# Layer 1's experts: the first matrix as the stationary operand, fetched for each block

## Chip, cores and metric

The kernel runs on one core of a Trainium2 chip. The metric is the device time of one execution in microseconds; the median of three runs is compared. One further execution was recorded by the hardware profiler, and all durations of single instructions come from it.

## What is computed

The reference is a decoder of two layers on 32 sequences of 100 tokens with 256 features, all in float32. Each layer has self-attention, cross-attention over a context of 361 rows, and a feed-forward part. The change concerns only the last part of all, the mixture of experts of layer 1, on 3200 tokens:

```python
def _L1_ffn_ref(x, shared_w1, shared_w2, experts_w1, experts_w2, gate_w):
    ...
    shared = jnp.einsum('td,dh->th', x_flat, shared_w1.T)
    shared = jnp.einsum('th,hd->td', jax.nn.silu(shared), shared_w2.T)
    gate_logits = x_flat @ gate_w.T
    top_k_gates, top_k_idx = jax.lax.top_k(gate_logits, TOP_K)
    top_k_gates = jax.nn.softmax(top_k_gates, axis=1)
    ...
    h = jnp.einsum('td,ehd->teh', x_flat, experts_w1)
    expert_out = jnp.einsum('teh,edh->ted', jax.nn.silu(h), experts_w2)
    selected = jnp.einsum('ted,te->td', expert_out, gates)
    return (shared + selected).reshape(B, S, D)
```

There are 8 experts with a hidden width of 1024. Each token uses two of them, with gates from a softmax over its two largest logits, and a shared expert works on every token.

## The kernel before

Everything ahead of layer 1's feed-forward part is left as it is. The tokens are normalized and gated while layer 1's cross-attention runs; an indirect DMA (`send`) puts each token's row, with its gates and its number, twice into `sorted_dram`, once for each of its experts, so that the rows of one expert lie together. What follows has two stages, each with its order of instructions written out by hand for PE, DVE, ACT and SP (`in_order(SP)`).

**The stage of the shared expert** (the pool `f1s`) walks over 13 chunk pairs h of 256 tokens (the last has 128) times 8 slices m of the hidden width. `hidden` (its matmuls are booked on L208, inside `project`) multiplies a slice of the first matrix, as the stationary operand, by the turned tokens; ACT applies the silu (L1839); `added` multiplies by the second matrix (L1847). The stage begins with `rows_of`, which loads normalized rows (`xn`, L1799), and `rows_turned`, which turns them on PE (L1812). Along the way SP loads the experts' matrices: all eight first matrices into `wx1` (64 KB in each partition, L1928) and all eight second matrices into `wx2` (L1969). `blocks_of` works out which expert each block belongs to (`number`) and where its rows start (`rows_at`), and `get` fetches the first blocks' rows (`xg`, L1778). Some constants (L1748 to L1761: `ti`, `ones8`, `pi`, `empty` and others) are made by POOL in the pool `f1r`, which is opened after `wx1`. `empty` is written to the spare rows of `acc_dram` (L1914) and `sorted_dram` (L1915).

**The stage of the experts** (the pool `f1u`) walks over TILES = 57 blocks of 128 rows, each of one expert; which one is only known from a register. For each block:

- `get` (SP) fetches the rows, four blocks ahead, into one of six buffers `xg`;
- `turned` (PE L1982, DVE L1986) turns the rows into `xgT`, two blocks ahead;
- `first` (PE L208, `sc<-wx,xgT`) has the turned rows as the stationary operand and 512 columns of the first matrix as the moving one, at an address in `wx1` that a register gives; ACT's silu (L2000) writes `h`, with tokens in the partitions;
- `hidden_turned` turns `h` with eight transposes on PE (L2009) into `hgT`; ACT (L2015) and DVE (L2017) copy one half each out of PSUM;
- `second` (PE L208, `po<-wx,hgT`) multiplies by the second matrix of the expert; DVE scales by the gate into `y` (L2032, three buffers); POOL's indirect DMA (L2033) adds the rows to `acc_dram`. Each such scatter waits for the one before it, and a buffer `xg` is free only when its scatter has ended, since the scatter reads the row numbers in it.

The loop sets the order on every engine:

```python
for t in range(-2, TILES):
    if 0 <= t + 4 < TILES and t >= 0:
        get(t + 4)
    if t + 2 < TILES:
        turned(t + 2)
    if t >= 0:
        hidden_turned(t)
    if 0 <= t + 1 < TILES:
        first(t + 1)
    if t >= 0:
        second(t)
```

At the end `acc_dram` is copied to the output.

Of the kernel before, what the change touches and what calls it, by code (L numbers as in the profile page):

```python
# [10 lines left out]
F32 = mybir.dt.float32  # L11
# [3 lines left out]
AF = mybir.ActivationFunctionType  # L15
# [3 lines left out]
P = 128  # L19
# [7 lines left out]
E = 8  # L27
HID = 1024
NTOK = B * T
NCH = NTOK // 128  # L30
TILES = (2 * NTOK + E * 127) // 128
# [35 lines left out]
def kernel(ctx: ExitStack, tc: tile.TileContext, io: dict, out: bass.AP):  # L67
    nc = tc.nc
# [22 lines left out]
    def mm_tile():  # L91
        return psum["mm"][1].tile([P, 512], F32, tag="mm", name="mm")
# [5 lines left out]
    ident = const.tile([P, P], F32, name="ident")  # L98
# [395 lines left out]
    w1 = open_weights(1)  # L494
# [584 lines left out]
    with tc.tile_pool(name="a1", bufs=2) as pool, tc.tile_pool(name="a1p", bufs=1) as fixed:  # L1079
# [4 lines left out]
        for k, shift in enumerate((np.pi / 2, 0.0)):  # L1084
            a = fixed.tile([P, 16], F32, tag=f"ang{k}", name=f"ang{k}")
            t = fixed.tile([P, 16], F32, tag=f"turns{k}", name=f"turns{k}")
# [14 lines left out]
        for c in range(2):  # L1101
            ps = mm_tile()
# [5 lines left out]
        ps = mm_tile()  # L1108
# [629 lines left out]

    wx1_cm = tc.tile_pool(name="wx1", bufs=1, side="right")
    wx1_pool = wx1_cm.__enter__()
    wx1 = wx1_pool.tile([P, E, 2, HID], F32, name="wx1")
    fixed_cm = tc.tile_pool(name="f1r", bufs=1, side="right")
    fixed = fixed_cm.__enter__()
    w1s, w2s = loaded
# [20 lines left out]
    number = fixed.tile([1, TILES], I32, name="number1")  # L1767
# [2 lines left out]
    blocks_cm = tc.tile_pool(name="f1t", bufs=2, side="right")  # L1770
    blocks = blocks_cm.__enter__()
    xgs = {}

    def get(t):

        xg = blocks.tile([P, ROW], F32, tag="xg", name="xg", bufs=6)
        at = nc.sync.value_load(rows_at[0:1, t : t + 1], min_val=0, max_val=E * RG)
        load = nc.sync.dma_start(xg, sorted_dram[bass.ds(at, P), :])  # L1778
        for put in sent:
            tc.add_manual_dep(  # L1780
                load.ins, put.name,
                mybir.DependencyInfo(
                    mybir.DependencyClass.Sync, mybir.DependencyReason.DATA
                ),
                reason="all rows are there",
            )
        xgs[t] = xg

    with tc.tile_pool(name="f1s", bufs=2, side="right") as pool, in_order(SP):
# [28 lines left out]
        def chunks(h):  # L1818
            return range(2 * h, min(2 * h + 2, NCH))
# [36 lines left out]
        def store(h):  # L1856
            n = len(chunks(h))
            nc.sync.dma_start(
                acc_dram[256 * h : 256 * h + n * P, :].rearrange("(c p) d -> p c d", p=P),
                accs.pop(h)[:, :n, :],  # L1860
            )
# [62 lines left out]
        for n in range(len(units) + 2):  # L1924
            if n < len(units):
                h, m = units[n]
                if m == 2 and 0 < h < E + 1:
                    nc.sync.dma_start(  # L1928
                        wx1[:, h - 1], io["f1_w1"][h].rearrange("(c p) n -> p c n", p=P)
                    )  # L1930
                if m == 4 and h % 2 == 1 and h // 2 + 1 < NB:
                    rows_turned(h // 2 + 1)
                    if h // 2 + 2 < NB:
                        rows_of(h // 2 + 2)
                hidden(h, m)
            if n >= 2:
                added(*units[n - 2])
            if n >= 8 and n % 8 == 4:
                store(n // 8 - 1)
                if n // 8 + 2 < NHB:  # L1940
                    sum_rows(n // 8 + 2)
            if n in (4, 8, 12, 14):
                gating(pool, NG - 1, {4: 2, 8: 3, 12: 4, 14: 5}[n])
            if n == 18:
                blocks_of()
            if n >= 16 and n % 2 == 0 and n < 32:

                nc.gpsimd.tensor_copy(pace, hTs[units[n]][0:1, 0:1])
                for k in range(2):
                    b = B - G + (n - 16) // 2  # L1950
                    if n < 24:
                        put(send(b, k))
                    else:
                        e = n - 24 + k
                        put(nc.gpsimd.indirect_dma_start(
                            sorted_dram[:, :],
                            bass.IndirectOffsetOnAxis(ap=rest[:, e : e + 1], axis=0), empty, None,
                        ))
            if n == 40:

                xpool_cm.__exit__(None, None, None)
                norms_cm.__exit__(None, None, None)
                early_cm.__exit__(None, None, None)
                wx2_cm = tc.tile_pool(name="wx2", bufs=1)
                wx2_pool = wx2_cm.__enter__()
                wx2 = wx2_pool.tile([P, E, 8, D], F32, name="wx2")
            if n >= 42 and n % 6 == 0 and n // 6 < 7 + E:
                e = n // 6 - 7
                nc.sync.dma_start(  # L1969
                    wx2[:, e], io["f1_w2"][e + 1].rearrange("(c p) n -> p c n", p=P)  # L1970
                )
            if n == 92:
                for t in range(4):
                    get(t)
        store(NHB - 1)
    with tc.tile_pool(name="f1u", bufs=2, side="right") as pool, in_order(SP):
        xgTs, hgTs, experts_ = {}, {}, {}

        def turned(t):
            pt = mm_tile()  # L1980
            for c in range(2):
                nc.tensor.transpose(  # L1982
                    pt[:, c * P : (c + 1) * P], xgs[t][:, c * P : (c + 1) * P], ident
                )
            xT = blocks.tile([P, 2, P], F32, tag="xgT", name="xgT")
            nc.vector.tensor_copy(xT.rearrange("p c t -> p (c t)"), pt[:, : 2 * P])  # L1986
            xgTs[t] = xT
            experts_[t] = nc.tensor.value_load(number[0:1, t : t + 1], min_val=0, max_val=E - 1)

        def first(t):  # L1990

            e, xT = experts_[t], xgTs.pop(t)
            ps = sc_tile()
            for n in range(2):
                project(
                    ps[:, n, :], [xT[:, c, :] for c in range(2)],
                    [wx1[:, bass.ds(e, 1), c, n * 512 : (n + 1) * 512] for c in range(2)],
                )
            h = pool.tile([P, HID], F32, tag="h", name="h")
            nc.scalar.activation(h, ps.rearrange("p a b -> p (a b)"), AF.Silu)  # L2000
            hgTs[t] = h

        def hidden_turned(t):
            h = hgTs[t]
            hT = pool.tile([P, 8, P], F32, tag="hgT", name="hgT")
            for n in range(2):
                pt = mm_tile()
                for m in range(4):
                    nc.tensor.transpose(  # L2009
                        pt[:, m * P : (m + 1) * P], h[:, (4 * n + m) * P : (4 * n + m + 1) * P],  # L2010
                        ident,
                    )
                dst = hT[:, 4 * n : 4 * n + 4, :].rearrange("p m t -> p (m t)")
                if n == 0:
                    nc.scalar.copy(dst, pt)  # L2015
                else:
                    nc.vector.tensor_copy(dst, pt)  # L2017
            hgTs[t] = hT

        def second(t):  # L2020
            e, hT, xg = experts_.pop(t), hgTs.pop(t), xgs.pop(t)
            po = po_tile()
            project(
                po[:, :D], [hT[:, m, :] for m in range(8)],
                [wx2[:, bass.ds(e, 1), m, :] for m in range(8)],
            )
            g = pool.tile([P, 1], F32, tag="gx", name="gx")
            ge = pool.tile([P, E], F32, tag="ge", name="ge")
            nc.vector.tensor_tensor(ge, xg[:, D : D + E], onehot[:, t, :], ALU.mult)
            nc.vector.tensor_reduce(g, ge, AX.X, ALU.add)  # L2030
            y = pool.tile([P, D], F32, tag="y", name="y", bufs=3)
            nc.vector.tensor_scalar(y, po[:, :D], g, None, ALU.mult)  # L2032
            nc.gpsimd.indirect_dma_start(  # L2033
                acc_dram[:, :],
                bass.IndirectOffsetOnAxis(
                    ap=xg[:, D + E : ROW].bitcast(U32), axis=0
                ),
                y, None, compute_op=ALU.add,
            )

        for t in range(-2, TILES):
            if 0 <= t + 4 < TILES and t >= 0:
                get(t + 4)
            if t + 2 < TILES:
                turned(t + 2)
            if t >= 0:
                hidden_turned(t)
            if 0 <= t + 1 < TILES:
                first(t + 1)
            if t >= 0:  # L2050
                second(t)
# [2 lines left out]
    wx2_cm.__exit__(None, None, None)  # L2054
    blocks_cm.__exit__(None, None, None)
    fixed_cm.__exit__(None, None, None)
    wx1_cm.__exit__(None, None, None)
    close_weights(5)
    share_psum()

# [119 lines left out]
```

## Time and profile before

| | |
|---|---|
| median of 3 runs | 3895.03 us (3892.2 to 3896.37) |
| the profiled execution | 3894.81 us, of which its span is 3893.1 |
| busy in the span | PE 3583.1, PEld 2250.5, DVE 2034.2, ACT 1523.8, POOL 1338.3 us |
| stage of the shared expert | from about 3225 to 3417 us of the span |
| loop over the blocks | from 3419.2 to 3875.6 us |
| output copied | from 3880 us to the end |

PE is TensorE's matmuls, PEld its weight loads, which overlap the matmuls; DVE, ACT, POOL and SP are VectorE, ScalarE, GpSimd and SyncE. A line of a timeline gives the start and the duration in microseconds, then engine, line of the kernel, operation and the tiles as output<-inputs, with the number of instructions merged; what stands in square brackets is the idle time ahead of it and what ended it. The end of a matmul is modelled by the profiler, so that the recorded durations of neighbours overlap; the distance from one start to the next is the time that a matmul takes in a row. A tile's buffer number is left out, so `wx` stands for both `wx1` and `wx2`. "q" behind an engine marks its queue issuing a DMA.

### The profile page before, as it was taken

What the parts mean: (1) busy time and instruction counts of PE and PEld (TensorE: products, weight loads), DVE (VectorE), ACT (ScalarE), POOL (GpSimd) and SP (SyncE); (2) the same over time, 40 slices, a digit from 0 to 9 for tenths busy, and PEclk for the clock granted to TensorE, in tenths of its full rate; (3) what the DMA queues carried; (4) which work ended last, traced back from release to release, by engine and by line L of the source; (5) the groups of instructions that cost most, each with busy time, mean ns of one, the idle gap of its engine ahead of it and who ended that gap; (6) DMA issues with size and microseconds to landing.
All of it is one profiled execution on the core that took longest, in us unless ns stands there. A gap on an engine that the chain in (4) does not pass through costs nothing. (4 is left out here: it accounts for less than half of the span.)

```text
span 3893.1 us, 65394 instructions
## 1 busy us (share of the span) xinstructions
PE 3583.1 (92%) x25610; PEld 2250.5 (58%) x25610; DVE 2034.2 (52%) x5647; ACT 1523.8 (39%) x3254; POOL 1338.3 (34%) x941
## 2 busy tenths in 40 slices
PE   7888999996889899799999999999999998999998
PEld 5665565654545453333356666666666667867665
DVE  6776666654677766565544554645545552012221
ACT  4554555552322220456644444444444442222111
POOL 3334666664444532101122333332333332011211
PEclk9999999998899999899999999999999999999999
DMA  2001000000000000100100000000000004412222
GB/s 79 2 2 58 18 20 20 18 5 15 1 1 1 1 1 0 42 1 1 34 9 16 19 21 22 17 23 19 21 23 18 26 11 145 163 31 34 34 35 58
DMA packets 86508, 103.70 MB, mean 27 GB/s; under 512 B 13374, under 2 KB 79494, under 8 KB 85610
## 3 DMA queue, kind: packets, MB, share of 16 engines
q1 hardware_dynamic: 71532, 80.80, 7.1%
q0 software_dynamic: 12688, 15.36, 2.4%
q8 instruction: 205, 3.36, 0.4%
q10 hardware_dynamic: 1982, 3.35, 0.3%
q14 instruction: 101, 0.83, 0.1%
HBM read 74.02 MB, written 28.71 MB: 26 GB/s over the span
## 5 line engine op out<-in xcount | busy, mean ns | idle before, releaser
L1600 POOL TENSOR_TENSOR ex<-ex,rc 100x1444 f32<-100x1444 f32 x128 | 331.5, 2590 | 633.5 <-DVE rc L1599 631.0
L1591 ACT ACTIVATE ex<-s,nmx 100x361 f32<-100x361 f32 x512 | 303.1, 594 | 284.8 <-DVE nmx L1582 228.9
L364 POOL TENSOR_TENSOR s<-s,nmx 100x800 f32<-100x800 f32 x128 | 194.7, 1522 | 375.3 <-DVE nmx L363 372.0
L1199 ACT ACTIVATE h<-sc,cols 128x800 f32<-128x800 f32 x256 | 222.1, 923 | 135.1 <-PE sc L1193 134.8
L208 PE MATMUL mm<-f_we,x1T 128*100 128x512 f32 x512 | 265.5, 649 | 4.3 <-DVE x L1009 2.2
L2033 POOL DMA_INDIRECT acc_dram<-y,xg x57 | 88.8, 1557 | 494.3 <-DVE y L2032 342.8
L1582 DVE CUSTOM_DVE_ANT_0 s<-sc,mb 100x361 f32<-100x361 f32 x512 | 250.3, 526 | 0.7 <-PE sc L1575 0.6
L1575 PE MATMUL sc<-kT,qT 64*100 64x361 f32 x1024 | 206.3, 480 | 46.3 <-DVE vb L1563 30.7
L208 PE MATMUL po<-wx,hgT 128*128 x912 | 206.3, 379 | 0.3 <-ACT hgT L2015 0.3
L208 PE MATMUL sc<-wx,xgT 128*128 x456 | 205.2, 593 | 0.8 <-DVE xgT L1986 0.8
L208 PEld LDWEIGHTS po<-wx,hgT 128*128 128x128 f32 x912 | 173.3, 190 | 47.8 <-issue 26.8
L2032 DVE TENSOR_SCALAR y<-po,gx 128x256 f32<-128x256 f32 x57 | 27.6, 484 | 330.9 <-PE po L208 330.9
L1548 PE MATMUL sc<-x_wa,cT 128*128 128x512 f32 (+1 forms) x512 | 188.2, 490 | 0.0
L1022 DVE SCALAR_TENSOR_TENSOR x<-mm,wt,x 100x256 f32<-100x256 f32 x256 | 123.6, 483 | 114.2 <-PE mm L208 107.7
L376 PE MATMUL mm<-ident,ex 100*100 100x100 f32 x1024 | 126.5, 262 | 58.9 <-ACT eT L385 22.9
L1625 PEld LDWEIGHTS po<-eT,vb 128*64 128x64 f32 (+1 forms) x3072 | 140.2, 140 | 69.0 <-issue 68.6
L1518 PE MATMUL mm<-cT,x_wa 128*128 128x361 f32 x512 | 176.3, 467 | 0.0
L171 POOL TENSOR_TENSOR rs<-va,neghalf 100x4 f32<-100x4 f32 (+1 forms) x96 | 92.9, 970 | 220.1 <-DVE va L170 218.2
L385 ACT COPY eT<-mm 100x400 f32<-100x400 f32 x192 | 92.3, 492 | 193.9 <-PE mm L376 193.7
L1607 PE MATMUL mm<-ident,ex 100*128 100x100 f32 (+1 forms) x1536 | 164.3, 257 | 4.2 <-POOL ex L1600 4.1
L1614 ACT COPY eT<-mm 128x400 f32<-128x400 f32 (+1 forms) x256 | 125.9, 492 | 105.6 <-PE mm L1607 105.5
L1625 PE MATMUL po<-eT,vb 128*64 128x100 f32 (+1 forms) x3072 | 165.9, 258 | 0.0
(347 smaller groups left out, 7607.0 us busy)
## 6 DMA issues: line engine op xcount, KB each, us to landing
wx<-in_f_w SPq DMA_DIRECT2D x16, 1024.0 KB
xg<-sorted_dram SPq DMA_DIRECT2D x57, 132.5 KB
cb<-in_ctx SPq DMA_DIRECT2D x32, 192.0 KB
cT<-in_ctxT SPq DMA_DIRECT2D x32, 180.5 KB
cT<-in_ctxT SPq DMA_DIRECT2D x64, 90.2 KB
x<-in_x SPq DMA_DIRECT2D x8, 400.0 KB
x_dram<-x SPq DMA_DIRECT2D x32, 100.0 KB
xn_dram<-x SPq DMA_DIRECT2D x8, 400.0 KB
```

What stands on the lines that cost most here:

```text
L208: nc.tensor.matmul(ps, lhsT[k], rhs[k], start=(k == 0), stop=(k == n - 1))
L364: nc.gpsimd.tensor_tensor(sm, sm, bc(nmx, 2, T), ALU.add)
L376: nc.tensor.transpose(pt[:T, j * T : (j + 1) * T], exs[s, r // 2][:, 4 * (r % 2) + j, :], ident[:T, :T],)
L1199: nc.scalar.activation(h1, both[r2][:, :, :GT], AF.Tanh, bias=col("a1_b1", o))
L1518: nc.tensor.matmul(kTs[u][c][:, :S2], x1_wa[:, m * P : (m + 1) * P], cT[:, 0, :], start=True, stop=False,)
L1548: nc.tensor.matmul(ps[:kn, e, :n], cT[:, 0, at], x1_wa[:, 1024 + c0 : 1024 + c0 + n], start=True, stop=False,)
L1575: nc.tensor.matmul(ps[:T, e, :S2], qT[p0 : p0 + 64, m, tok], kT[p0 : p0 + 64, c, :], start=True, stop=True,)
L1582: nc.vector.tensor_tensor_reduce(s[:, e, :], ps[:T, e, :S2], mb, 1.0, 3.4e38, ALU.add, ALU.min, nmx[:, e : e + 1],)
L1591: nc.scalar.activation(ex[:, 2 * c + e, :], s[:, e, :], AF.Exp, bias=nmx[:, e : e + 1], scale=-1.0, accum_out=sm[:, 2 * c + e : 2 * c + e ...
L1600: nc.gpsimd.tensor_tensor(ex, ex, bc(rc, 2, S2), ALU.mult)
L1607: nc.tensor.transpose(pt[:kn, j * T : (j + 1) * T], ex[:, j, k0 : k0 + kn], ident[:T, :T])
L1625: nc.tensor.matmul(po[64 * e : 64 * e + 64, m * T : (m + 1) * T], vb[k][:kn, 256 * (u % 2) + 64 * h : 256 * (u % 2) + 64 * h + 64], eT[:kn ...
```

## The change

The first product of an expert's block is computed the other way round. Slices of 128 columns of the first matrix become the stationary operand and the turned rows the moving one, so that the product comes out with the hidden width in the partitions, as the second product needs it. The silu writes `hgT` directly, and `hidden_turned` with its transposes and two copies is gone. Each block's first matrix (1 MB) is fetched anew from memory by SP, at an address that a register gives (`first_matrix`), three blocks ahead into one of four buffers `w1b`; the tile `wx1` and its eight loads during the shared expert's stage are gone. With `wx1` gone, the pool `f1r` and what follows it lie at other addresses.

```diff
-    wx1_cm = tc.tile_pool(name="wx1", bufs=1, side="right")
-    wx1_pool = wx1_cm.__enter__()
-    wx1 = wx1_pool.tile([P, E, 2, HID], F32, name="wx1")
...
+    w1_of = {}
+
+    def first_matrix(t):
+
+        e = nc.sync.value_load(number[0:1, t : t + 1], min_val=0, max_val=E - 1)
+        w1 = blocks.tile([P, 2, HID], F32, tag="w1b", name="w1b", bufs=4)
+        nc.sync.dma_start(
+            w1, io["f1_w1"][1 : E + 1][bass.ds(e, 1)].rearrange("o (c p) n -> p (o c) n", p=P)
+        )
+        w1_of[t] = w1
...
-                if m == 2 and 0 < h < E + 1:
-                    nc.sync.dma_start(
-                        wx1[:, h - 1], io["f1_w1"][h].rearrange("(c p) n -> p c n", p=P)
-                    )
...
             if n == 92:
                 for t in range(4):
                     get(t)
+                    if t < 3:
+                        first_matrix(t)
...
         def first(t):
 
-            e, xT = experts_[t], xgTs.pop(t)
+            w1, xT = w1_of.pop(t), xgTs.pop(t)
             ps = sc_tile()
-            for n in range(2):
+            for m in range(8):
                 project(
-                    ps[:, n, :], [xT[:, c, :] for c in range(2)],
-                    [wx1[:, bass.ds(e, 1), c, n * 512 : (n + 1) * 512] for c in range(2)],
-                )
-            h = pool.tile([P, HID], F32, tag="h", name="h")
-            nc.scalar.activation(h, ps.rearrange("p a b -> p (a b)"), AF.Silu)
-            hgTs[t] = h
-
-        def hidden_turned(t):
-            h = hgTs[t]
+                    ps[:, m // 4, m % 4 * P : m % 4 * P + P],
+                    [w1[:, c, m * P : (m + 1) * P] for c in range(2)],
+                    [xT[:, c, :] for c in range(2)],
+                )
             hT = pool.tile([P, 8, P], F32, tag="hgT", name="hgT")
-            for n in range(2):
-                pt = mm_tile()
-                for m in range(4):
-                    nc.tensor.transpose(
-                        pt[:, m * P : (m + 1) * P], h[:, (4 * n + m) * P : (4 * n + m + 1) * P],
-                        ident,
-                    )
-                dst = hT[:, 4 * n : 4 * n + 4, :].rearrange("p m t -> p (m t)")
-                if n == 0:
-                    nc.scalar.copy(dst, pt)
-                else:
-                    nc.vector.tensor_copy(dst, pt)
+            nc.scalar.activation(
+                hT.rearrange("p m t -> p (m t)"), ps.rearrange("p a b -> p (a b)"), AF.Silu
+            )
             hgTs[t] = hT
...
         for t in range(-2, TILES):
             if 0 <= t + 4 < TILES and t >= 0:
                 get(t + 4)
+            if 3 <= t + 3 < TILES:
+                first_matrix(t + 3)
             if t + 2 < TILES:
                 turned(t + 2)
-            if t >= 0:
-                hidden_turned(t)
             if 0 <= t + 1 < TILES:
                 first(t + 1)
```

## The prediction

> **What bounds the kernel now.** I read the rows of busy tenths first, then the table of stages for the loop over expert blocks and for the stretch before it, then the groups by shape in that loop, then one block in order of time.
>
> ```profile
> PE   7888999996889899799999999999999998999998
> ...
> GB/s 79 2 2 58 18 20 20 18 5 15 1 1 1 1 1 0 42 1 1 34 9 16 19 21 22 17 23 19 21 23 18 26 11 145 163 31 34 34 35 58
> ```
> ```profile
> 3419.20:3875.60 456.40, 455.13 (x1934) 319.12 (x1934) 98.13 (x282) 91.68 (x114) 87.21 (x56) 1.00 0.21 32
> ```
> ```profile
> 3300.00:3400.00 100.00, 100.00 (x477) 88.25 (x476) 6.89 (x10) 23.21 (x59) 0.00 (x0) 1.00 0.52 175
> ```
> The columns of the last two lines are the stretch, its length, busy time of PE, PEld, DVE, ACT and POOL, granted clock, DMA share and GB/s. The block loop lasts 456.4 us and PE is busy 455.1 of them at full clock; DVE, ACT and POOL are each busy under a quarter, and the DMA engines 21%. PE bounds this loop. A busy PE could hide waits, so I check the spacing of one block:
>
> ```profile
> 3503.67 0.38 PE L1982 MATMUL mm<-ident,xg 128*128 128x128 f32 x2
> 3503.89 1.04 PE L2009 MATMUL mm<-ident,h 128*128 128x128 f32 x8
> 3504.63 1.55 POOL L2033 DMA_INDIRECT acc_dram<-y,xg  x1 [6.42 <-DVE y L2032]
> 3504.76 3.60 PE L208 MATMUL sc<-wx,xgT 128*128 x8
> 3508.19 3.62 PE L208 MATMUL po<-wx,hgT 128*128 x16
> 3508.56 0.33 SPq L1778 DMA_DIRECT2D xg<-sorted_dram  x1
> 3511.65 0.38 PE L1982 MATMUL mm<-ident,xg 128*128 128x128 f32 x2
> ```
> From start to start, two transposes of the rows take 0.22 us, eight transposes of the hidden values 0.87, the first product's eight passes 3.43 (0.429 each), the second product's sixteen 3.46 (0.216 each): 7.98 us, with no hole. One FP32 matmul stands in the trace as two passes. Whatever changes the block's time has to change PE's passes, or make PE wait.
>
> **What the Trainium skill says.** "TensorE: Matmul & The Clock Gate", section "LDWEIGHTS (loading the stationary operand)", prices a load by its columns: 128 columns at 1.2 per ns, an estimated 107 ns. The trace books 190 ns for one, but loads start closer than that. The same page, "Back-to-back issue gap", says that a stream of load and matmul pairs is paced by both, which is the question here. "DMA: Bandwidth & Descriptors", "Issuing engines are not separate DMA queues", says that all DMAs share the 16 engines, so the new fetches and the scatters meet there. Its "Queues, rings and completion order" has each engine change between queues only after a whole packet of descriptors. No view of before shows that sharing at the new load.
>
> **The change, part by part.**
>
> *First product.* Removed: 4 matmuls of 512 columns, 8 passes x 0.429 = 3.43 us a block. Added: 8 x 2 matmuls of 128 columns, 32 passes. The columns streamed are the same, 32 x 128 = 8 x 512, but there are 32 weight loads for 8, and a load may no longer hide under a pass. The nearest rows:
>
> ```profile
> 1581.36 0.97 PEld L208 LDWEIGHTS mm<-xm,a_w 128*128 128x128 f32 x8 [2.26 <-DVE xm L1151]
> ```
> ```profile
> 3411.88 0.61 PE L208 MATMUL mm<-xT,w 128*128 128x128 f32 x4
> ...
> 3412.33 0.60 PE L1847 MATMUL sc<-w,hT 128*128 128x256 f32 x2
> ...
> 3412.76 0.61 PE L208 MATMUL mm<-xT,w 128*128 128x128 f32 x4
> ```
> Eight full loads with 4-column matmuls, so with nothing to hide under, span 0.97 us: (0.97 - 0.19) / 7 = 0.111 us each. That is the pace of loads alone, near the page's 107 ns, and the booked 190 ns overlap. The second fence has the very shape of the new passes, in the shared expert's last half chunk: 4 of them take 3412.33 - 3411.88 = 0.45 us, 0.112 each. I take 0.111: 32 x 0.111 = 3.55 us, so **+0.12 a block**. Bounds: 0.107 (0.429 / 4, no cost of the extra loads) gives 0.00, and 0.1125 gives +0.17.
>
> *Transposes of the hidden values* (`hidden_turned`): 8 x 0.109 = **-0.87 us a block**, all on PE's path.
>
> *Evacuations.* ACT's copy (0.585) and DVE's copy (0.691) of each block go; the silu keeps its 1024 elements (1.02 us) and writes the turned form at once. ACT and DVE were never waited for in the steady block, so this is worth nothing there. Its cover is the second product of the block before (3.46 us) ahead of the silu's reader; were it gone, 1.0 us would show.
>
> *Fetching the matrix.* SP issues, per block, a register load, register arithmetic and a 1 MB transfer more. Six `get` in a row are issued within 5.79 us (from 3400.09 in SP's timeline), 1.1 us each; a fetch has one register sum more, so both make some 2.4 of a block's 7.2. Removed: eight 1 MB issues at 3231 to 3345, where PE did not wait for them. The loop before held 0.21 DMA share; 1.05 MB at 175 / 0.52 = 337 GB/s adds 3.1 us per block. Together (0.21 x 7.98 + 3.1) / 7.23 = 0.66 of the DMA engines. The order of instructions puts `first_matrix(t + 3)` on SP right behind `get(t + 4)`, which waits for the scatter of block t - 2; SP's gather at 3508.56 follows the y of 3504.35 by 4.2 us. Hence the fetch goes out about 5 us into block t - 1 and is needed at the start of `first(t + 3)`, three blocks on: 3 x 7.23 - 5 = 17 us for a transfer of about 3 to 6. **Cost 0**, by that cover. Queued behind SP's wait are only the next gather and fetch, with the same lead. The first three fetches go out from 3401, between the gathers, 15 us before the loop; also covered.
>
> *Scatter.* It must finish before the next one starts. POOL's issue at 3504.63 to SP's release by 3508.56 is 3.9 us, in a period of 8.0. If it stood behind a whole fetch it would take 3.9 + 3.1 = 7.0, still under 7.23, but barely.
>
> *Fill and drain.* The 57 blocks last 456.5 us, from the first pass at 3419.16 to the last y at 3875.64; 57 x 7.98 = 454.9, so 1.6 are edges, of which 0.99 is PE waiting for the first silu ahead of L2009 and goes. After: 57 x (0.22 + 3.55 + 3.46 = 7.23) = 412.1, with 0.5 of edges 412.6. **-43.9 us.**
>
> *The seam ahead of the shared expert.* Without the 64 KB `wx1`, the constants (L1748 to L1761) lie where memory is free early: the order shows POOL's seven instructions (1.3 us together) behind the memset of L1100, where POOL then idles 13.97 us, and `acc_dram<-empty` ahead of SP's first context loads (0.34 us there, used 18 us later). Both cost nothing. At the seam SP's first `xn` load no longer stands behind the last `x_dram` store:
>
> ```profile
> 3227.24 0.43 SPq L1799 DMA_DIRECT2D xn<-xn_dram  x1
> ...
> 3233.30 1.09 PE L1812 MATMUL mm<-ident,xn 128*128 128x128 f32 x4 [8.57 <-DMA xn<-xn_dram]
> ```
> PE waits 8.57 us for it. It can be issued near 3225.2, when the last tiles of the stage before come free: **-2 us** (0 to -2.5); next to be late is the rest of the same load.
>
> *Sum*: -43.9 - 2 = -45.9. The profiled execution took 3894.8 (span 3893.1 and 1.7 around it), 0.2 under the median of the runs, so 3895.0 - 45.9 = **3849**. With the bounds: pace 0.107 and the whole seam 3841, pace 0.1125 and no seam 3854.
>
> **Rivals.**
> *Slower, by the scatter.* It shares the DMA engines with a fetch that is new in every block, and the scatters are a serial chain. If one takes over 8.0 us instead of 3.9, POOL's chain sets the block and the kernel is slower; at 9.0 it is 57 x 1.0 = +57, 3952. For it: the chain lies on POOL and DMA, and a fetch ahead of it is new. Against: 3.9 + 3.1 = 7.0 needs the worst meeting each time. A chance of 4 in 100; a chain of 7.3 to 7.9 only eats part of the gain, 3855 to 3887, and with late fetches at the loop's start I give that 12 in 100.
> *Slower, by the weight loads.* If loads in a long row ran at the booked 0.190, the first product would take 6.08 and the block 9.76: +1.78 x 57 = +101, 3996. It decides from (8.01 - 3.46 - 0.22) / 32 = 0.135 a pass. The row of eight at 0.111 speaks against it; 32 in a row are not in the trace. 3 in 100.
> *No difference.* The gain of 0.76 a block is lost to waits by chance: 2 in 100.
> The likeliest case, PE bound at 7.2 to 7.3 a block, keeps 79 in 100.
>
> **How the numbers follow.** 3849 is the likeliest case. The range 3840 to 3864 holds it and the mildest of the partial losses, up to 0.25 us a block (57 x 0.25 = 14 above the sum). A measurement of this kernel tells about 0.2%, 8 us, from no change: faster 0.91, within 0.02, slower 0.07.
>
> **What would show it.** Right: blocks 7.2 to 7.3 apart, the new passes 0.111 apart, L2009 gone, PE with no wait for the fetched tile, PE's wait at the seam near 6.5. Wrong: passes over 0.13 apart; PE or PEld waiting for `w1b`; `acc_dram` scatters over 7 us apart from y to release, or y waiting for a scatter.

## The result, and the profile after

The changed kernel takes 3851.9 us (median of 5 runs, 3843.5 to 3857.1), the kernel before 3895.7 beside it (5 runs, 3892.2 to 3900.2). The ratio is 0.9885, with a 95% interval from 0.9869 to 0.9901: 43.8 us less, where the prediction had 45.9 less. The profiled execution of the changed kernel took 3857.05 (span 3855.3); it is the slowest of the five, so its span is not read as the kernel's time.

The rows of busy tenths and of GB/s come first again.

```profile
PE   7888999996898989799989999999999999999997
...
GB/s 80 2 2 55 20 18 20 18 9 15 1 1 1 1 1 1 43 1 1 1 39 15 16 23 20 21 23 16 24 19 21 24 15 53 134 160 175 182 177 162
```
In the last slices PE is as full as it was, and the bytes moved there rise from about 35 to 160 to 180 GB/s: these are the fetches. The table of stages, for the block loop and for the shared expert, in the columns used in the prediction:

```profile
3422.00:3836.40 414.40, 413.56 (x2846) 386.27 (x2846) 58.82 (x227) 58.43 (x57) 87.05 (x56) 1.00 0.61 170
```
```profile
3300.00:3400.00 100.00, 100.00 (x477) 88.20 (x476) 6.89 (x10) 23.33 (x60) 0.00 (x0) 1.00 0.40 132
```
The loop lasts 414.4 us for 456.4, PE is still busy in all but 0.8 of it, and it is PE's work that has shrunk. The DMA share rose from 0.21 to 0.61 meanwhile. The shared expert's stage, whose eight loads went, is as long per instruction as before: 477 matmuls in 100 us, now as then. PE's rows of one block, in order of time:

```profile
3505.32 0.38 PE L1988 MATMUL mm<-ident,xg 128*128 128x128 f32 x2
3505.54 3.74 PE L208 MATMUL sc<-xgT,w1b 128*128 128x128 f32 x32
3509.11 3.62 PE L208 MATMUL po<-wx,hgT 128*128 x16
3512.57 0.38 PE L1988 MATMUL mm<-ident,xg 128*128 128x128 f32 x2
```
From start to start: two transposes 0.22, the 32 new passes 3.57 (0.1116 each), the second product 3.46, together 7.25 us. The eight transposes of 0.87 are not there. The groups by shape in the loop, where the number after the bar is busy time and then the mean of one in ns:

```profile
L208 PE MATMUL sc<-xgT,w1b 128*128 128x128 f32 x1824 | 213.2, 275 | 0.5 <-DVE xgT L1992 0.4
L208 PEld LDWEIGHTS sc<-xgT,w1b 128*128 128x128 f32 x1824 | 208.2, 192 | 1.2 <-DVE xgT L1992 0.6 <-issue 0.5
```
1824 is 57 x 32. A load is booked with 192 ns and still one comes every 112; in front of all 1824 matmuls PE stood idle for 0.5 us, none of which the profile puts down to `w1b` (two waits for it that are too short to be listed are found below).

The balance of the two profiled executions, 3893.1 to 3855.3 = -37.8 us, has five entries. The loop, from its first pass to the last y, went from 456.5 to 414.4: -42.0. The wait at the seam ahead of the shared expert went from 8.6 to 4.4: -4.2. From the last y to the end it is 18.9 for 17.4: +1.5. The stage of the shared expert, without that wait, is 0.2 shorter. The rest, +7.2, lies ahead of all this: PE reaches the seam at 3231.9, before at 3224.7 (the start of the next row less its wait). It doesn't follow the edits: in the nine runs below the last pass of the stage before the seam starts anywhere from 3219.8 to 3230.8. So I take it for a spread from run to run, which the medians even out.

### The profile page after: what moved, and what is told of

The parts are those of the page before. It is cut to its first block, busy times and chain, and to the rows that moved or that the text cites. A ratio compares the mean times of both kernels' runs of the same rounds, so it can differ in the third digit from the quotient of the medians.

```text
span 3855.3 us, 67089 instructions
## 1 busy us (share of the span) xinstructions
PE 3549.4 (92%) x26522; PEld 2320.8 (60%) x26522; DVE 1995.5 (52%) x5590; ACT 1492.0 (39%) x3197; POOL 1338.7 (35%) x941
## 3 DMA queue, kind: packets, MB, share of 16 engines
q8 instruction: 211, 3.46, 0.4%
## 5 line engine op out<-in xcount | busy, mean ns | idle before, releaser
L208 PE MATMUL sc<-xgT,w1b 128*128 128x128 f32 x1824 | 213.2, 275 | 0.5 <-DVE xgT L1992 0.4
L208 PEld LDWEIGHTS sc<-xgT,w1b 128*128 128x128 f32 x1824 | 208.2, 192 | 1.2 <-DVE xgT L1992 0.6
L2007 ACT ACTIVATE hgT<-sc 128x1024 f32<-128x1024 f32 x57 | 58.4, 1025 | 351.3 <-PE sc L208 351.3
## 6 DMA issues: line engine op xcount, KB each, us to landing
xg<-sorted_dram SPq DMA_DIRECT2D x57, 132.5 KB
```

The source lines that it names most:

```text
L208: nc.tensor.matmul(ps, lhsT[k], rhs[k], start=(k == 0), stop=(k == n - 1))
```

## Experiments

The theory: PE's passes are the whole gain, the fetch costs PE nothing, the copies were free, and the seam gives some microseconds. Against it stood a fetch whose cost is only hidden because something else shrank, and, after the trace of the changed kernel, the chain of scatters. All times are medians, each with its ratio to the kernel before on the same chip.

### One part alone

**The transposes put back**, into a PSUM tile that nobody reads, in the changed kernel:

```diff
+        def dummy_turned(t):
+            for n in range(2):
+                pt = mm_tile()
+                for m in range(4):
+                    nc.tensor.transpose(
+                        pt[:, m * P : (m + 1) * P], hgTs[t][:, 4 * n + m, :], ident
+                    )
...
+            if t >= 0:
+                dummy_turned(t)
             if 0 <= t + 1 < TILES:
                 first(t + 1)
```

> The changed kernel with eight transposes of 128 columns per block put back on PE, turning hgT into PSUM where nobody reads them, without the two copies. Theory (PE's passes set the block): 8 x 0.109 = 0.87 us more per block, blocks 8.12 apart, loop near 464 us, 57 x 0.87 = +50 us on the changed kernel, near 3902. Rival (the copies on ACT and DVE were what cost): no change, near 3852. Rival (the scatters' chain sets the block at 7.1 to 7.25 and PE has slack): less than +42, near 3885 to 3893.

Measured: 3898.7 us, ratio 1.000 [0.9991, 1.0008]. PE's rows in order of time:

```profile
3501.14 0.38 PE L1988 MATMUL mm<-ident,xg 128*128 128x128 f32 x2
3501.36 1.04 PE L2016 MATMUL mm<-ident,hgT 128*128 128x128 f32 x8
3502.23 3.74 PE L208 MATMUL sc<-xgT,w1b 128*128 128x128 f32 x32
...
3509.26 0.38 PE L1988 MATMUL mm<-ident,xg 128*128 128x128 f32 x2
```
The block is 8.12 us, 7.25 + 0.87, and the loop 463.9. With eight transposes that nobody reads the whole gain is gone: 463.9 - 413.85 = 50 us more than the loop of the next run, for 57 x 0.87 = 49.6. So PE's passes are what the loop's gain is made of. (The loop is even 7.4 us longer than before, since the new first product takes 0.14 us a block more; the seam gives 4.2 of that back, and the rest is within the spread of the runs.)

**The two copies put back**, with the same halves of 128x512 into a spare tile:

```diff
+        def dummy_copies(t):
+            spare = pool.tile([P, 8, P], F32, tag="spare", name="spare")
+            nc.scalar.copy(spare[:, 0:4, :].rearrange("p m t -> p (m t)"), hgTs[t][:, 0:4, :].rearrange("p m t -> p (m t)"))
+            nc.vector.tensor_copy(spare[:, 4:8, :].rearrange("p m t -> p (m t)"), hgTs[t][:, 4:8, :].rearrange("p m t -> p (m t)"))
...
+            if t >= 0:
+                dummy_copies(t)
```

> The changed kernel with two copies of 128 x 512 per block put back, one on ACT and one on DVE, from hgT into a spare tile that nobody reads (from SBUF, where the former ones read PSUM). Theory (PE's passes set the block): nothing within 4 us, near 3852, blocks 7.25 apart. Rival (the copies cost): the sum of both, 0.585 + 0.691 = 1.28 us x 57 = +73, or the longer one alone, +39.

Measured: 3850.4 us, ratio 0.9879 [0.9862, 0.9895]; a loop of 413.85 us. The copies cost nothing, as costed. These read SBUF where the former ones read PSUM, and nobody waits for them: the run shows that ACT and DVE have the room, not what a wait for a copy would cost.

**The fetch alone**: the kernel before with `first_matrix` in place of `wx1`, the turned rows still stationary, the transposes still there:

```diff
                 project(
                     ps[:, n, :], [xT[:, c, :] for c in range(2)],
-                    [wx1[:, bass.ds(e, 1), c, n * 512 : (n + 1) * 512] for c in range(2)],
+                    [w1[:, c, n * 512 : (n + 1) * 512] for c in range(2)],
                 )
```

> The fetch of the first matrix for each block as in the changed kernel, with the product, the transposes and the copies as before (w1b is the moving operand). Theory (the fetch costs PE nothing, the seam gives 4 us): blocks 7.98 apart, loop 456 to 457 us, PE's wait for xn near 4.5 us, total 3891 to 3893. Rival (the fetch delays blocks): blocks over 8.05 apart, total over 3900.

Measured: 3892.3 us, ratio 0.9985 [0.9978, 0.9993]. The stage table for its loop:

```profile
3415.10:3872.00 456.90, 454.75 (x1934) 318.71 (x1932) 98.68 (x283) 91.67 (x114) 87.02 (x57) 1.00 0.56 154
```
The loop from its first pass to the last y is 456.48 us, the same to a hundredth as in the kernel before, with 0.56 of the DMA engines busy for 0.21. What it gains outside is the seam, of which more below.

**The turned product alone**: the kernel before with `wx1` kept, stationary, and no transposes:

```diff
-            for n in range(2):
+            for m in range(8):
                 project(
-                    ps[:, n, :], [xT[:, c, :] for c in range(2)],
-                    [wx1[:, bass.ds(e, 1), c, n * 512 : (n + 1) * 512] for c in range(2)],
+                    ps[:, m // 4, m % 4 * P : m % 4 * P + P],
+                    [wx1[:, 0, c, m * P : (m + 1) * P] for c in range(2)],
+                    [xT[:, c, :] for c in range(2)],
                 )
```

> The kernel before with the turned product only: all first matrices stay in wx1 as before, and every block takes the first expert's as its stationary operand, whatever its expert [...], so the values of the other experts are left out. Theory (all of the loop's gain is PE's): blocks 7.25 apart, loop 414 us as in the changed kernel, without the gain at the seam, so 3852 + 4 = 3856; the scatter starts 0.28 us after y in every block and its round is 3.9 us again. Rival (the fetch and its meeting with the scatters cost part of the gain): blocks under 7.2, total under 3850.

Measured: 3856.5 us, ratio 0.9894 [0.9878, 0.9911].

```profile
3450.00:3700.00 250.00, 250.00 (x1722) 233.95 (x1721) 35.71 (x136) 35.83 (x35) 53.19 (x34) 1.00 0.24 38
```
Its loop is 413.87 us with a DMA share of 0.24, that of the run with the copies 413.85 with the fetches in it. In these runs the fetch is therefore worth zero from both sides; the next part finds 0.6 us of it in the changed kernel. This run keeps PE's old wait at the seam (8.7 us for 4.3), which is most of its distance to the 3850.4 of the run with the copies.

### The chain of scatters

In the profiled execution of the changed kernel the loop has 0.6 us more than in the run with the copies, in two blocks of 7.49 and 7.60 us. Looking for these I found, as the normal course, the meeting that the prediction had used as its worst case. The waits of POOL in the loop (total, times, longest), of the changed kernel:

```profile
POOL acc_dram L2025 <- issue: 222.3, 39, 8.3
...
POOL acc_dram L2025 <- DVE y L2024: 71.0, 13, 6.0
```
Only 13 scatters start when their y is there; 39 start with nothing in the profile to release them, which by the order of events is the end of the scatter before. SP's and POOL's rows in the timeline:

```profile
3603.69 0.33 SPq L1786 DMA_DIRECT2D xg<-sorted_dram  x1
...
3604.30 1.55 POOL L2025 DMA_INDIRECT acc_dram<-y,xg  x1 [5.48 <-issue]
3604.86 0.38 SPq L1777 DMA_DIRECT2D w1b<-in_f_w  x1
...
3610.81 0.33 SPq L1786 DMA_DIRECT2D xg<-sorted_dram  x1
...
3611.42 1.55 POOL L2025 DMA_INDIRECT acc_dram<-y,xg  x1 [5.56 <-issue]
3611.98 0.38 SPq L1777 DMA_DIRECT2D w1b<-in_f_w  x1
```
Read it as a circle. A scatter that ends releases two things: SP's gather, which wants the `xg` buffer of that scatter (3610.81), and POOL's next scatter (3611.42). Behind the gather SP issues the fetch (3611.98), while POOL still prepares the scatter. In the packet records of the round before, the fetch's 256 rows of 4 KB move from 3605.90 to 3609.67, the scatter's 128 rows of 1 KB from 3609.26 to 3610.35. Without a fetch a scatter's rows begin to move 2.1 us after its start (3504.63 to 3506.75 in the kernel before); the fetch's begin after 1.6 us, and so come first. So each scatter that ends sends out the transfer that the next scatter then stands behind: 7.1 us a round (3604.30 to 3611.42).

That is the usual round, not the mean. From the 12th scatter to the 53rd the mean is 7.39 us, since 16 of these 41 rounds took over 7.3 and one 9.9; what makes those longer, no run shows. PE's block is 7.25, so the scatters fell behind, from 2.6 to 8.1 us after the end of their y. The fetches fell behind with them: at the 12th block a fetch was issued 15.9 us ahead of its first pass, at the 51st 6.1.

```profile
3774.99 0.39 SPq L1777 DMA_DIRECT2D w1b<-in_f_w  x1
...
3781.08 3.65 PEld L208 LDWEIGHTS sc<-xgT,w1b 128*128 128x128 f32 x32 [0.21 <-issue]
3781.11 3.81 PE L208 MATMUL sc<-xgT,w1b 128*128 128x128 f32 x32
```
The last packet of this fetch ended at 3780.63, 0.48 us ahead of the pass, and that of the 55th block's 0.58 ahead. In the run with half of the second product, below, most blocks wait for the matrix, and there the distance is 0.43 to 0.6 us. The 51st and the 55th are the very blocks ahead of which PE is late, so I read the 0.6 us as PE waiting for the fetch. The lead of three blocks was used up just as the loop came to its end.

The Trainium skill, "DMA: Bandwidth & Descriptors", "Queues, rings and completion order", lets a DMA engine leave a queue only after a whole packet, typically of some 9 to 17 descriptors. A fetch has 272 records in the trace (256 rows and 16 small ones); spread evenly over 16 engines that is 17 for each, by this estimate about one such packet. The order of the records agrees with that; where packets of descriptors end is in no record, so the reason is argued, not shown.

If the circle is real, it must bind once PE is faster than its rounds. **Half of the second product left out**:

```diff
-                po[:, :D], [hT[:, m, :] for m in range(8)],
-                [wx2[:, bass.ds(e, 1), m, :] for m in range(8)],
+                po[:, :D], [hT[:, m, :] for m in range(4)],
+                [wx2[:, bass.ds(e, 1), m, :] for m in range(4)],
```

> The changed kernel with only four of the eight hidden slices in the second product (half of the sum is left out), so PE has 8 x 0.216 = 1.73 us less per block. Theory (the scatters' chain, with the fetch that SP issues behind each scatter, runs at 7.1 us and is next to bind): blocks 7.1 apart, loop near 406, total near 3844, y late because its buffers wait for scatters. Rival (PE still binds and the scatters adapt): blocks 5.5 apart, loop near 316, total near 3753.

Measured: 3838.8 us, ratio 0.9855 [0.984, 0.987], the scatters 7.09 us apart (median) where PE's passes need 5.52 a block. From the stage table, the waits and the timeline:

```profile
3450.00:3700.00 250.00, 207.27 (x1469) 192.51 (x1468) 36.68 (x140) 35.34 (x36) 54.31 (x35) 0.97 0.65 184
```
```profile
POOL acc_dram L2025 <- issue: 244.4, 44, 7.0
...
PE sc L208 <- DMA w1b<-in_f_w: 54.1, 31, 2.9
```
```profile
3601.44 1.55 POOL L2025 DMA_INDIRECT acc_dram<-y,xg  x1 [5.46 <-issue]
...
3608.52 1.55 POOL L2025 DMA_INDIRECT acc_dram<-y,xg  x1 [5.53 <-issue]
```
PE is busy 207 of 250 us and waits 31 times for the fetched matrix (the expectation had `y` waiting for its buffers instead); these two scatters are 7.08 apart. No engine is full, the DMA engines are at 0.65, and a chain sets the time. The first eight blocks, which live on the lead of their fetches, still come at PE's pace, so that the loop takes 396.6 us and not 406. From the ninth on a block takes 7.25 in the mean, no less than in the changed kernel, though PE has 1.73 us less to do.

**The same with ten `xg` buffers for six**, so that the gather, and the fetch behind it, no longer wait for the scatter just ended:

```diff
-        xg = blocks.tile([P, ROW], F32, tag="xg", name="xg", bufs=6)
+        xg = blocks.tile([P, ROW], F32, tag="xg", name="xg", bufs=10)
```

> As half_second, with ten buffers xg for six, so that SP's gather doesn't wait for the last scatters and the fetch behind it is released by PE's first product in place of a scatter. Theory (the chain is long because SP sends each fetch at the moment that a scatter ends, just ahead of the next one): blocks well under 7.1, 5.5 to 6.3 apart, total 3753 to 3800. Rival (fetch and scatter share the DMA engines and meet whatever the order): blocks stay near 7.1, total near 3844.

Measured: 3751.9 us, ratio 0.9632 [0.9617, 0.9647].

```profile
3450.00:3700.00 250.00, 250.00 (x1902) 238.44 (x1902) 47.22 (x180) 46.64 (x46) 70.19 (x45) 1.00 0.84 238
```
The block is 5.52, PE is full again, and the DMA engines now bear a share of 0.84. One number of buffers is worth 3838.8 - 3751.9 = 86.9 us; in the profiled executions the loop takes 315.4 us for 396.6. So it was neither bandwidth nor the length of a scatter in itself, but what a scatter releases.

**Ten `xg` buffers in the changed kernel itself**, the same line alone:

> The changed kernel with ten buffers xg for six. Theory (PE binds; the chain of the scatters lies just under): the scatter starts 0.3 us after y in nearly all blocks in place of up to 8 us after, the two blocks of 7.49 and 7.60 go, and the total is the same within 3 us, near 3851. Rival (the late scatters cost the changed kernel time): 5 us or more faster.

Measured: 3851.0 us, ratio 0.988 [0.9865, 0.9895] (4 runs); loop 413.85, every block 7.25. Its waits, and the time of a scatter from issue to landing (the median from 3450 to 3700 us, in the changed kernel, then here):

```profile
POOL acc_dram L2025 <- DVE y L2024: 292.1, 52, 5.7
```
```profile
acc_dram<-y,xg POOLq DMA_INDIRECT x34, 6.3
```
```profile
acc_dram<-y,xg POOLq DMA_INDIRECT x34, 3.8
```
Now 52 scatters wait for their y and for nothing else, and they land in 3.8 us, with 0.66 of the DMA engines busy for 0.63. In total time it can't be told from the changed kernel, whose late fetches cost 0.6 us in the execution that was profiled. It is the version to build on, since here the fetches keep a lead of 25 us to the end.

**Half the fetch**, together with half the second product and six buffers, asks whether the fetch ahead of the scatter is what makes the round long:

```diff
-        w1 = blocks.tile([P, 2, HID], F32, tag="w1b", name="w1b", bufs=4)
+        w1 = blocks.tile([P, 1, HID], F32, tag="w1b", name="w1b", bufs=4)
...
-            w1, io["f1_w1"][1 : E + 1][bass.ds(e, 1)].rearrange("o (c p) n -> p (o c) n", p=P)
+            w1, io["f1_w1"][1 : E + 1][bass.ds(e, 1), :P].rearrange("o (c p) n -> p (o c) n", p=P)
...
-                    [w1[:, c, m * P : (m + 1) * P] for c in range(2)],
+                    [w1[:, 0, m * P : (m + 1) * P] for c in range(2)],
```

> As half_second with its six buffers xg, but each fetch brings only the first 512 KB of the matrix, and the first product uses that half for both of its sums (the other half is left out; the number of passes is the same). In half_second the blocks were 7.0 apart, and a fetch and its gather kept the DMA engines 3 to 5 us in each round. Theory (the round is long because a scatter's rows wait behind the whole fetch): the round shrinks by about half a fetch, 1.4 to 1.9 us, to 5.1 to 5.7, and PE's 5.5 binds nearly everywhere, total 3750 to 3770. Rival (the round is made of fixed latencies of semaphores and of the scatter itself): blocks stay near 7.0 apart, total near 3839.

Measured: 3768.8 us, ratio 0.9669 [0.9653, 0.9685]; the scatters 5.79 us apart (median), blocks of 5.80 in the mean. POOL's rows:

```profile
3599.97 1.55 POOL L2025 DMA_INDIRECT acc_dram<-y,xg  x1 [4.14 <-DVE gx L2022]
3605.92 1.55 POOL L2025 DMA_INDIRECT acc_dram<-y,xg  x1 [4.40 <-DVE gx L2022]
3612.16 1.55 POOL L2025 DMA_INDIRECT acc_dram<-y,xg  x1 [4.70 <-DVE gx L2022]
```
The releaser that the profile names here, the gate `gx`, did not end these waits: it belongs to a later block, since from the 15th block to the 53rd the scatters start 6.0 to 8.6 us after the end of their own y. So the circle is still there and still sets the time, with a shorter round, 5.79 for 7.09. These 1.30 us are what the fetch became shorter: from its first packet to its last it takes 2.45 us for 3.74 (medians of the 13th to the 53rd), and a scatter lands in 5.1 us for 6.4. The expectation had taken half of the fetch's time, 1.4 to 1.9 us, and PE binding nearly everywhere; with 1.30 the round stays above PE's 5.52, and from the 20th block on PE waits for the fetch.

### The seam

**The pool of constants opened ahead of `wx1`** in the kernel before, nothing else:

```diff
-    wx1_cm = tc.tile_pool(name="wx1", bufs=1, side="right")
-    wx1_pool = wx1_cm.__enter__()
-    wx1 = wx1_pool.tile([P, E, 2, HID], F32, name="wx1")
     fixed_cm = tc.tile_pool(name="f1r", bufs=1, side="right")
     fixed = fixed_cm.__enter__()
...
+    wx1_cm = tc.tile_pool(name="wx1", bufs=1, side="right")
+    wx1_pool = wx1_cm.__enter__()
+    wx1 = wx1_pool.tile([P, E, 2, HID], F32, name="wx1")
```

> The kernel before with the pool f1r opened ahead of wx1, so that only the constants lie where memory is free early. Theory (the seam's gain comes from the constants' place, which lets SP send the first xn load ahead of the last x_dram store): PE's wait for xn falls from 8.6 to 4.5 us, and the total by about 4 us, near 3891. Rival (it comes from the place of xn or from the missing loads of wx1): 8.6 us and 3895 as before.

Measured: 3893.4 us, ratio 0.9993 [0.9984, 1.0001] (13 runs). The seam in the changed kernel, then in this one:

```profile
3232.07 0.39 SPq L1807 DMA_DIRECT2D xn<-xn_dram  x1
...
3233.21 0.29 SPq L1643 DMA_DIRECT2D x_dram<-x  x1
...
3236.32 1.94 PE L1820 MATMUL mm<-ident,xn 128*128 128x128 f32 x8 [4.38 <-DMA xn<-xn_dram]
```
```profile
3228.87 0.39 SPq L1799 DMA_DIRECT2D xn<-xn_dram  x1
...
3230.01 0.29 SPq L1643 DMA_DIRECT2D x_dram<-x  x1
...
3233.08 1.94 PE L1812 MATMUL mm<-ident,xn 128*128 128x128 f32 x8 [4.33 <-DMA xn<-xn_dram]
```
In both the load of the rows now stands ahead of the last `x_dram` store on SP, 0.1 us after PE's last pass, and PE waits 4.3 to 4.4 us for 8.6. So the seam's gain belongs to where the constants lie, not to the new product or the fetch. In total time it shows as 2.8 us, with an interval that takes in zero.

## Why the prediction was right, step by step

| step | predicted | measured |
|---|---|---|
| one new pass | 0.111 us | 0.1116 |
| a block | 7.23 us | 7.25 |
| the loop | -43.9 us | -42.0 in the profiled pair, 456.48 - 413.85 = -42.6 in the other runs |
| the two copies | 0 | 0 (413.85 with them) |
| the fetch | 0 | 0 (456.48 for 456.48, 413.85 for 413.87); 0.6 in the changed kernel's trace |
| the lead of a fetch | 17 us | 15.9 at the 12th block, 6.1 at the 51st |
| share of the DMA engines | 0.66 | 0.61 |
| the seam | -2 us (0 to -2.5) | -4.2 in the trace |
| a scatter | 3.9 us, 7.0 at the worst | 6.5 from its start to SP's release; rounds of 7.1, in the mean 7.39 |
| the sum | -45.9 us | -43.8 by the medians |

**First product and transposes.** The step that decided was the price of a pass with a load of its own. It was read from four passes of the same shape in the shared expert and eight loads in a row elsewhere, and 32 in a row, 57 times over, keep that pace. The rival by the weight loads, with 0.19 a pass, is refuted by 1824 passes. 0.02 us a block was missed, 1.1 us in all.

**Evacuations and fetch.** Both zeros held within 0.6 us. The lead of 17 us was worked out for a fetch behind a scatter that starts with its y. In the profiled execution the scatters are late, every round over 7.25 comes off the lead, and PE used it up at the 51st and the 55th block.

**The seam** is the term that was mis-sized: PE was to wait 6.5 us there, and waits 4.4. The prediction moved the load's issue and left its landing as it was. The issue came 2.5 us after PE's last pass (3227.24, with PE idle from 3233.30 - 8.57 = 3224.73) and now comes 0.1 after it: -2.4, the end of its range. The other -1.8 is the landing, 6.06 us from issue to PE's start before (3227.24 to 3233.30) and 4.25 after (3232.07 to 3236.32). Before, `x_dram<-x`, `acc_dram<-empty` and `sorted_dram<-empty`, 100, 128 and 132.5 KB, were moved in that stretch ahead of it; they no longer stand there. That they are the reason is argued from the order; no run took them away one by one.

**The scatter** is the step whose reasoning failed, though not the number. "Needs the worst meeting each time" treated the meeting of fetch and scatter as chance. It isn't: the fetch waits, through the gather's buffer, for the scatter ahead of the one that it meets, so once the scatters lag the meeting comes in every round. The prediction named that very release when it worked out the fetch's lead, and didn't carry it over to the scatter. Nor was 7.0 the worst case. It counts to SP's release, which came after 6.5, and leaves out the 0.6 us from there to the next scatter's start; that makes the usual round of 7.1, and some took up to 9.9. A chain of 7.3 to 7.9, which the prediction gave 12 in 100, is what the profiled execution had in the mean (7.39). Two of the signs of being wrong came too: scatters over 7 us from y to release and, in two blocks, PE waiting for the fetch.

The number held because the fetches' lead took up the long rounds, and 57 blocks were just few enough for it. The prediction had counted that lead for the fetch alone, not as a reserve against a slow chain, so this part of its success is luck. With the lead gone, each further block would have cost up to 7.39 - 7.25 = 0.14 us, an estimate from the two means.

What stays open is what starts the circle and what makes some rounds longer. The execution of the changed kernel that was profiled is in it from the twelfth block on; with the copies put back, which change nothing for SP or POOL, nearly all scatters start 0.3 us after their y. How many of the executions without a profile were in it is not known.

## What to carry to other kernels

Choose the operand to be turned, or loaded, by the form in which the next product needs the result: passes with 128 moving columns cost only 4% more per column here than passes of 512 (0.1116 x 4 = 0.446 for 0.429), so a product that comes out turned for that price replaces its transposes. Before a load is put behind a wait on one queue, ask who releases that wait, and whether the load delays the next release: a few more buffers broke such a circle here, worth nothing that shows in the changed kernel and 87 us once PE was faster. Read the lead of a transfer at the end of a loop and not only at its start: a chain that is a little slower than the engine eats it before it costs time. When a large tile goes from a kernel, look at what moves into its place: the seam's 4.2 us came from where a few constants lay, not from the eight loads that went.

## What the runs showed of the hardware

A load of 128x128 in float32 is booked with 192 ns and repeats every 112 ns, so PEld's 93% in the loop (386.27 of 414.40) says no more about room on PE than the 70% before did: PE had none in either. And the DMA engines carried 238 GB/s at a share of 0.84 under a PE that never waits, while with the same transfers in a circle 184 GB/s at 0.65 made PE wait for a sixth of its time (42.7 of 250 us): a low share does not say that transfers are hidden. A scatter of 128 rows of 1 KB lands in 3.8 us, and in 6.3 when a fetch of 1 MB goes out just ahead of it.
